# Attention times a gated FFN on one Trainium2 core: features in rows for x, gate and result

## Chip, cores and metric

One core of a Trainium2 chip. The metric is the device time of one execution in microseconds (us): the median of three runs for the kernel before, and beside it one profiled execution, from which all durations below are taken. PE is TensorE (PEld its weight loads), DVE is VectorE, ACT is ScalarE, POOL is GpSimd, SP is SyncE, which does nothing here but issue DMAs.

## What is computed

x is [8, 512, 256]: B = 8 sequences of T = 512 tokens with E = 256 features.

```python
xn = layernorm(x)                              # over the features, no weights
q, k, v = split(xn @ in_proj_w.T)              # 16 heads of 16
q, k = rope(q), rope(k)
mask = (delta >= 0) & (delta < 250)            # causal, a window of 250
s = softmax(where(mask, q k^T / 4, min)) v @ out_proj_w.T
h = relu(s0 * [xn, -xn] @ W0) * 2              # W0, W1, W2 hold +1 and -1
h = relu(s1 * h @ W1) * 2                      # 256 -> 1024 -> 1024 -> 256
g = silu(s2 * h @ W2)
result = x + s * g
```

## The kernel before

**Tiles.** A tile has 128 rows (partitions). A sequence is NT = 4 token tiles; its features are EC = 2 chunks of 128. Matmuls put the token axis or the feature axis in the rows of their result according to which operand is the stationary one. Before the change x is loaded with tokens in rows (load_x, L106), four tiles of 128 tokens by 256 features.

**One batch.**
- stats (L231): per token tile a bn_stats and a bn_aggr on DVE give mean and variance; DVE adds EPS and POOL takes the power -1/2 (L240).
- norm (L247): DVE writes xn = (x - mean) * rstd, both of them one number per row.
- turn_x (L255): two TensorE transposes per token tile (L268) bring xn into features-in-rows; DVE copies it to xT (L280; ACT in batch 0, L278), ACT writes the scaled fp16 part xh (L281), DVE the remainder xl (L284).
- project (L302): k and q, each in parts a and b, from xT [2 chunks, 512 tokens] into PSUM, times cosine and sine on DVE (L319), rotated on POOL (L339), split into a high and a low part (split_hi L353 on ACT, split_lo L359 on DVE), both written to DRAM and read back in another arrangement (stack, L366) with four heads in the rows. project_v (L288) gives v with tokens in rows.
- layer (L399): the two wide FFN layers, L415. Each product is one fp16 and one fp32r matmul per chunk, 512 columns; the result is split again by ACT (L426) and DVE (L424).
- last (L429): z = h2 @ W2 with tokens in rows, four tiles of 128x256, 16 matmuls each; DVE scales it into gate (L467). gate_ready (L493): exp on ACT, plus one on POOL, reciprocal on DVE (L503), product on POOL.
- attention: nine steps per batch. A step computes scores (L605), takes exp on ACT (L624), masks on POOL (L640, L647) and multiplies the step before with v (L679). keep (L690) gathers a group of heads, invert and divide (L752 on) make the quotients.
- project_o (L778): att @ w_o per token tile; x is loaded a second time (xr, L787), DVE multiplies by gate (L804), POOL adds xr (L809), SP stores.

**Order.** Nothing is left to a scheduler. Each piece of work is a triple (place, cost, function). run (L212) sorts the pieces by place, calls them in that order, and keeps a clock that is the sum of the costs of pieces so far. A function may return follow-ups with a delay; they are called when the clock has passed their due time. So a place in units of SEQ = 42 per batch says where in the instruction streams of all engines a piece stands, and a delay says how many units of TensorE work lie between. Each engine, SP too, runs its stream strictly in order. prepare (L374) gives the places for the next batch's stats, norm, x, k, q and v; ffn (L534) those of the layers; last_at and late (L512, L519) those of z and of project_o; attention (L720) puts the nine steps among the pieces by cost and places the stacks.

**Buffers.** ps_m has three PSUM banks, shared by transposes, projections, FFN tiles, z and project_o in rotation; ps_s has two buffers for scores (two banks each), ps_o one. xT, xh and xl, as well as the tile for part b of q and k, are single. The last batch (b = 7) does its second layer in two halves of 256 tokens, so that the first half's z can come early.

**The start.** Loads of x, the weights and the rope table go out at 0.8 to 4.4 us; kb0, kb1 and kb2 are the boolean weights as bytes, from which w0, w1 and w2 are made in two precisions on DVE, ACT and POOL (make_w0 L169, make_w1 L174, make_w2 L182). warm (L206) runs idle matmuls to keep TensorE busy until the first real ones.

**The end.** project_o of the last batch stands for token tiles 0 and 1 at unit 40, within the second half of the second layer, and for tiles 2 and 3 after z. The last tile is multiplied on POOL and DVE and stored by SP (out_of_psum, L792).

Of the kernel before, what the change touches and what calls it, by code (L numbers as in the profile page):

```python
# [34 lines left out]
def tile_attention_times_gated_ffn(  # L35
    ctx: ExitStack,
    tc: tile.TileContext,
    x: bass.AP,
    w_qkv: bass.AP,
# [6 lines left out]
    out: bass.AP,  # L46
):

# [75 lines left out]
    nc.scalar.dma_start(wqkv_sb, w_qkv.rearrange("(c p) f -> p c f", p=P))  # L124
# [18 lines left out]
    counts = const.tile([P, 3 * B], F32, name="counts")  # L143

# [24 lines left out]
    def make_w0(c):  # L169

        nc.vector.tensor_tensor(w0["h"][:, c], kb0[:, c], kb0[:, EC + c], ALU.subtract)
        nc.scalar.copy(w0["l"][:, c], w0["h"][:, c])
# [58 lines left out]
    def stats(b):  # L231
        st = states[b] = {}
        mv = small.tile([P, NT, 2], F32, tag="mv", name=f"mv_{b}")
        rstd = small.tile([P, NT], F32, tag="rstd", name=f"rstd_{b}")
        for t in range(NT):
            bn = small.tile([P, 6], F32, tag="bn", name=f"bn_{b}_{t}")
            nc.vector.bn_stats(bn, xs[b, t])
            nc.vector.bn_aggr(mv[:, t, :], bn)
        nc.vector.tensor_scalar(rstd, mv[:, :, 1], EPS, None, ALU.add)
        nc.gpsimd.tensor_tensor(rstd, rstd, minus_half, ALU.pow)  # L240
        nc.vector.scalar_tensor_tensor(
            mv[:, :, 1], mv[:, :, 1], LEAST_VAR, ones, ALU.is_ge, ALU.mult,
            accum_out=counts[:, 2 * B + b : 2 * B + b + 1],
        )
        st["mv"], st["rstd"] = mv, rstd

    def norm(b, t):  # L247
        st = states[b]
        xn = st["xn", t] = work.tile([P, E], F32, tag="xn", name=f"xn_{b}_{t}")
        nc.vector.tensor_scalar(  # L250
            xn, xs[b, t], st["mv"][:, t, 0:1], st["rstd"][:, t : t + 1],
            ALU.subtract, ALU.mult,
        )

    def turn_x(b, t, plain=False):  # L255

        st = states[b]
        xn = st.pop(("xn", t))
# [7 lines left out]
        pt = ps_m.tile([P, EC, P], F32, tag="mm", name=f"xnT_ps_{b}_{t}")  # L266
# [8 lines left out]
        def parts_():  # L275
            xT = st["xT"][:, :, ts(t, P)]
            if b == 0:
                nc.scalar.copy(xT, pt)  # L278
            else:
                nc.vector.tensor_copy(xT, pt)  # L280
            nc.scalar.mul(hi, pt, sgnx)  # L281

        def low():
            nc.vector.scalar_tensor_tensor(lo, pt, sgnx, hi, ALU.mult, ALU.subtract)  # L284

        return [(0.0, parts_), (0.5, low)]
# [15 lines left out]
    def project(b, what, part):  # L302
        st = states[b]
        col = E * "qk".index(what) + P * "ab".index(part)
        ps = ps_m.tile([P, T], F32, tag="mm", name=f"{what}{part}_ps_{b}")
# [11 lines left out]

        def times(i):
            nc.vector.tensor_tensor(  # L319
                m[:, i], ps, rope_sb[:, i if part == "a" else 1 - i], ALU.mult  # L320
            )

        def both():
            times(0)
            times(1)
            if part == "b":
                return [
                    (1.4, lambda: rotate(b, what)),
                    (4.0 if b else 7.0, lambda: split_hi(b, what)),
                    (5.1 if b else 8.2, lambda: split_lo(b, what)),  # L330
                ]

        return [(0.0, both)]
# [40 lines left out]
    def prepare(b, plain=False):  # L374

        if b == 0:
            at = dict(stats=-40, norm=-38, x=-36, k=0, q=3, v=9.2)
            dx, dp, dv = 1.0, 1.5, 1.5
        else:

            at = dict(stats=9 if b > 1 else 12, norm=14.5, x=16.5, k=22, q=25, v=SEQ + 0.6)
            dx, dp, dv = 1.5, 1.5, 1.0
            at = {n: SEQ * (b - 1) + f for n, f in at.items()}
        out = [(at["stats"], 0, lambda: stats(b))]
        for t in range(NT):
            out += [
                (at["norm"] + dx * t, 0, lambda t=t: norm(b, t)),
                (at["x"] + dx * t, 0.25, lambda t=t: turn_x(b, t, plain)),
                (at["v"] + dv * t, 0.87, lambda t=t: project_v(b, t)),
            ]  # L390
# [38 lines left out]
    def last(b, t, how):  # L429
        st = states[b]  # L430
        pz = ps_m.tile([P, E], F32, tag="mm", name=f"z_ps_{b}_{t}")
        if how == "at once":
            for c in range(NF1):
                nc.tensor.matmul(
                    pz, st["h2p"][:, c, ts(t, P)], w2["l"][:, c].bitcast(F32),
                    start=(c == 0), stop=(c == NF1 - 1),
                )
        else:
            for p in "hl":
                for c in range(NF1):  # L440
                    nc.tensor.matmul(  # L441
                        pz, st["h2" + p][:, c, ts(t, P)], w2[p][:, c],
                        start=(c == 0 and p == "h"), stop=(c == NF1 - 1 and p == "l"),
                    )
        gate = st["gate", t] = outs.tile([P, E], F32, tag=f"gate{t}", name=f"gate_{b}_{t}")
        if how == "final":
            den = denominator(b, t)

            def ends():
                nc.scalar.activation(den, pz, AF.Exp, scale=scales[:, 1:2])  # L450
                nc.vector.tensor_scalar(gate, pz, scales[:, 0:1], None, ALU.mult)
                return [(0.3, add)]

            def add():
                nc.scalar.activation(den, den, AF.Identity, bias=1.0)
                return [(0.3, invert_)]

            def invert_():
                nc.vector.reciprocal(den, den)
                if t + 1 < NT:  # L460
                    nc.gpsimd.tensor_tensor(gate, gate, den, ALU.mult)
                st["den"] = den
# [3 lines left out]
        def scale():  # L466
            nc.vector.tensor_scalar(gate, pz, scales[:, 0:1], None, ALU.mult)  # L467
            if how != "later":
                return [(0.5 if t == 0 else 4.5, lambda: gate_ready(b, t))]
# [20 lines left out]
    def denominator(b, t):  # L490
        return work.tile([P, E], F32, tag="den", name=f"den_{b}_{t}")

    def gate_ready(b, t):  # L493
        st = states[b]
        gate, den = st["gate", t], denominator(b, t)
        nc.scalar.activation(den, gate, AF.Exp, scale=-1.0)

        def add():
            nc.gpsimd.tensor_scalar(den, den, 1.0, None, ALU.add)  # L499
            return [(0.9, invert_)]  # L500

        def invert_():
            nc.vector.reciprocal(den, den)  # L503
            return [(1.8, lambda: nc.gpsimd.tensor_tensor(gate, gate, den, ALU.mult))]
# [7 lines left out]
    def last_at(b, t):  # L512

        if b + 1 < B:
            return SEQ * (b + 1) + 2 * L1 * (t + 1) + L3 * t
        half = t // 2
        return SEQ * b + NF0 * L1 + NT * L3 + HALF * (half + 1) - 2 * L3 + L3 * (t % 2)

    def late(b, t):  # L519

        if b + 1 == B and t >= NT // 2:
            return last_at(b, NT - 1) + L3 + 0.9 * (t - NT // 2)
        if b + 1 == B:
            return SEQ * b + 40.0 + 0.9 * t
        return SEQ * (b + 1) + (32.0 + 3.2 * t if b + 2 < B else 18.0 + 2.5 * t)

    def finish_ffn(b, t, how):
        quick.add(last_at(b, t))
        out = [(last_at(b, t), L3, lambda: last(b, t, how))]
        if how == "later":  # L530
            out.append((late(b, t) - 4.0, 0, lambda: gate_ready(b, t)))
        return out

    def ffn(b):  # L534
# [3 lines left out]
        for f in range(NF0):  # L538
# [3 lines left out]
            if f % 2 and b > 0:  # L542
                now += L3
# [176 lines left out]
    def attention(b, among):  # L720
# [17 lines left out]
        for g in range(NG):  # L738

            at = times[used[g - 2][-1]] + 0.01 if g > 1 else first - (10.0 if b else 2.0)  # L740
# [37 lines left out]
    def project_o(b, t, final=False):  # L778
        st = states[b]
        pp = ps_m.tile([P, E], F32, tag="mm", name=f"att_ps_{b}_{t}")  # L780
        for c in range(EC):
            nc.tensor.matmul(  # L782
                pp, st["V", c][:, ts(t, P)], wo_sb[:, c, :],
                start=(c == 0), stop=(c == EC - 1),
            )
        xr = work.tile([P, E], F32, tag="xr", name=f"xr_{b}_{t}")
        nc.sync.dma_start(xr, x[b, ts(t, P), :])  # L787
        st["xr", t] = xr
        if final and t + 1 == NT:
            att = work.tile([P, E], F32, tag="xn", name=f"att_{b}_{t}")  # L790

            def out_of_psum():  # L792
                y, den = st["gate", t], st["den"]
                nc.scalar.copy(att, pp)
                nc.gpsimd.tensor_tensor(y, y, att, ALU.mult)
                nc.vector.tensor_tensor(y, y, den, ALU.mult)
                nc.vector.tensor_tensor(y, y, xr, ALU.add)
# [206 lines left out]
```

## Time and profile before

| | |
|---|---|
| runs | 627.25, 627.94, 629.54 us; median 627.94 |
| profiled execution | 628.36 us, of which the span of the profile is 626.6 |
| granted TensorE clock, mean | 0.996 |
| busy DVE, ACT, POOL | 394.1, 299.7, 316.2 us |
| transposes xnT_ps (L268) | 64, median 273 ns each as recorded |
| xn (L250) | 32, mean 752 ns |
| xT copies on DVE (L280) | 28, mean 418 ns |
| z_ps (L441) | 512 matmuls of 256 columns |
| att_ps (L782) | 128 matmuls of 256 columns |
| DMA in all | 67.20 MB, mean 107 GB/s |

The recorded duration of a matmul includes its way through the array, and successive ones overlap; the time that TensorE spends on one is read from the distance of two starts, or from the chain of work. A wait is put down to the semaphore that came last.

### The profile page before, as it was taken

How to read it: one execution, taken by the hardware profiler on the slowest of the kernel's cores; microseconds unless marked ns; L12 is line 12 of the kernel's file. 1: busy time of each engine (PE TensorE's matmuls, PEld its weight loads, DVE VectorE, ACT ScalarE, POOL GpSimd, SP SyncE). 2: the span in 40 equal slices, each digit the busy share in tenths (PEclk: the TensorE clock that was granted, in tenths of full speed). 3: DMA queues.
4: the chain of work that ended last, by engine and by line, in shares of the span. 5: the costliest groups of instructions: out<-in, count | busy, mean ns of one | idle time of the engine just before them, and what ended most of it. 6: DMA issues, size and time to landing. Idle time of an engine off the chain costs nothing.

```text
span 626.6 us, 12051 instructions
## 1 busy us (share of the span) xinstructions
PE 608.6 (97%) x4842; PEld 398.4 (64%) x4842; DVE 394.1 (63%) x667; ACT 299.7 (48%) x441; POOL 316.2 (50%) x409
## 2 busy tenths in 40 slices
PE   8899999999999999999999999999999999999994
PEld 6455576556665567655676566765676556767793
DVE  6773535667575774766658576485665668456573
ACT  4566655534554445545354454453444544564411
POOL 2954542456533655427634366235662356638641
PEclk9999999999999999999999999999999999999998
DMA  9352721116311263114421252412532116230101
GB/s 273 117 197 95 260 85 51 51 68 216 122 51 51 87 208 110 52 51 172 139 93 51 75 214 76 143 33 86 208 94 88 51 69 227 77 109 19 53 18 48
DMA packets 38193, 67.20 MB, mean 107 GB/s; under 512 B 5104, under 2 KB 19184, under 8 KB 38128
## 3 DMA queue, kind: packets, MB, share of 16 engines
q1 hardware_dynamic: 36384, 64.24, 30.5%
q10 hardware_dynamic: 1744, 2.10, 1.0%
q8 instruction: 40, 0.66, 0.4%
q14 instruction: 25, 0.20, 0.1%
HBM read 36.96 MB, written 29.36 MB: 106 GB/s over the span
## 4 chain that ended last, share of the span: by engine, by line
PE 85%; DVE 5%; POOL 3%; DMA 3%; ACT 2%; issue 1%; SPq 0%; POOLq 0%; ACTq 0%; DVEq 0%
PE h_ps L415 41%; PE po L679 11%; PE z_ps L441 9%; PE sc L605 8%; PE v_ps L292 4%; PE att_ps L782 4%; PE qa_ps L307 2%; PE kb_ps L307 2%; PE qb_ps L307 2%; DMA kb<-in_k_dram 2%; PE ka_ps L307 2%; PE xnT_ps L268 1%; DVE den L503 1%; DVE h2l L424 1%; DVE xn L250 1%
## 5 line engine op out<-in xcount | busy, mean ns | idle before, releaser
L624 ACT ACTIVATE p<-sc 128x1024 f32<-128x1024 f32 (+2 forms) x144 | 138.5, 1013 | 75.0 <-PE sc L605 41.0
L415 PE MATMUL h_ps<-h1l,w1l_sb 128*128 128x512 f32 (+1 forms) x576 | 144.2, 392 | 0.0
L640 POOL TENSOR_SCALAR_AFFINE_SELECT p<-p 128x512 f32<-128x512 f32 x128 | 90.3, 711 | 104.0 <-ACT p L624 104.0
L415 PE MATMUL h_ps<-h1h,w1h_sb 128*128 128x512 f16 (+1 forms) x576 | 123.0, 356 | 0.5 <-ACT v_pad L299 0.5
L415 PEld LDWEIGHTS h_ps<-h1l,w1l_sb 128*128 128x128 f32 x576 | 99.5, 188 | 25.7 <-issue 6.8
L426 ACT ACTIVATE h2h<-h_ps 128x512 f16<-128x512 f32 (+1 forms) x72 | 39.6, 550 | 140.3 <-PE h_ps L415 140.2
L415 PEld LDWEIGHTS <-w1h_sb 128*128 128x128 f16 x576 | 51.5, 98 | 55.1 <-issue 13.4
L679 PE MATMUL po<-p,v_pad 128*32 128x378 f32 (+4 forms) x1216 | 77.2, 372 | 1.3 <-DVE S L703 1.1
L647 POOL TENSOR_SCALAR_AFFINE_SELECT p<-p 128x512 f32<-128x512 f32 (+1 forms) x96 | 50.0, 521 | 54.6 <-ACT p L624 49.7
L424 DVE SCALAR_TENSOR_TENSOR h2l<-h_ps,h2h 128x512 fp32r<-128x512 f32 (+1 forms) x72 | 44.3, 617 | 48.5 <-ACT h2h L426 48.5
L503 DVE RECIPROCAL den<-den 128x256 f32<-128x256 f32 x30 | 52.5, 1752 | 28.2 <-POOL den L499 28.1
L424 DVE SCALAR_TENSOR_TENSOR h1l<-h_ps,h1h 128x512 fp32r<-128x512 f32 x64 | 42.4, 675 | 34.8 <-ACT h1h L426 34.8
L605 PEld LDWEIGHTS sc<-q,k 32*128 32x128 f32 x1216 | 44.1, 184 | 26.1 <-issue 15.0
L754 DVE RECIPROCAL S<-S 128x128 f32<-128x128 f32 x64 | 58.9, 933 | 0.0
L426 ACT ACTIVATE h1h<-h_ps 128x512 f16<-128x512 f32 x64 | 38.2, 597 | 41.8 <-PE h_ps L415 41.2
L605 PE MATMUL sc<-q,k 32*128 32x378 f32 (+4 forms) x1216 | 57.2, 306 | 0.0
L415 PE MATMUL h_ps<-xl,w0l_sb 128*128 128x512 f32 x128 | 52.5, 491 | 0.0
L679 PEld LDWEIGHTS po<-p,v_pad 128*32 128x32 f32 x1216 | 31.3, 109 | 30.8 <-issue 16.2
L809 POOL TENSOR_TENSOR gate<-gate,xr 128x256 f32<-128x256 f32 x31 | 25.1, 810 | 46.8 <-DMA xr<-in_x_dram 41.2
L441 PE MATMUL z_ps<-w2l_sb,h2l 128*128 128x256 f32 x256 | 38.3, 291 | 0.4 <-DVE h2l L424 0.4
L415 PE MATMUL h_ps<-xh,w0h_sb 128*128 128x512 f16 x128 | 38.6, 383 | 0.0
L339 POOL TENSOR_TENSOR m_ka<-m_ka,m_kb 128x512 f32<-128x512 f32 x16 | 20.1, 1278 | 30.3 <-DVE m_kb L319 30.3
(97 smaller groups left out, 811.0 us busy)
## 6 DMA issues: line engine op xcount, KB each, us to landing
q<-dq SPq DMA_DIRECT2D x64, 256.0 KB, 3.6
dq<-qh SPq DMA_DIRECT2D x16, 512.0 KB, 3.4
dq<-m_qa SPq DMA_DIRECT2D x16, 512.0 KB, 5.0
k<-dk SPq DMA_DIRECT2D x32, 256.0 KB, 2.8
dk<-kh SPq DMA_DIRECT2D x8, 512.0 KB, 2.6
dk<-m_ka SPq DMA_DIRECT2D x8, 512.0 KB, 2.6
xr<-in_x_dram SPq DMA_DIRECT2D x32, 128.0 KB, 2.8
out_dram<-gate SPq DMA_DIRECT2D x32, 128.0 KB, 1.7
```

The costliest lines, as they stand in the source:

```text
L307: nc.tensor.matmul(ps, wqkv_sb[:, c, ds(col, P)], st["xT"][:, c, :], start=(c == 0), stop=(c == EC - 1),)
L415: nc.tensor.matmul(ph, w[p][:, c, ts(f, P)], st[src + p][:, c, cols], start=(k == 0), stop=(k == n - 1),)
L424: nc.vector.scalar_tensor_tensor(lo, ph, 0.0, hi, ALU.max, ALU.subtract)
L426: high = lambda: nc.scalar.activation(hi, ph, AF.Relu)
L441: nc.tensor.matmul(pz, st["h2" + p][:, c, ts(t, P)], w2[p][:, c], start=(c == 0 and p == "h"), stop=(c == NF1 - 1 and p == "l"),)
L503: nc.vector.reciprocal(den, den)
L605: nc.tensor.matmul(sc[r // 2][:, r % 2, ds(off, n)], st["k0", g][row, ts(j, P)], st[f"q{turn}", g][row, ds(j * P + first, n)], start=(turn ...
L624: nc.scalar.activation(p[:, 2 * half : 2 * half + 2, :n], sc[half][:, :, :n], AF.Exp, scale=D ** -0.5,)
L640: nc.gpsimd.affine_select(out=block, in_=block, compare_op=ALU.is_ge, fill=0.0, base=0, pattern=[[0, 4], [1, P]], channel_multiplier=-1,)
L647: nc.gpsimd.affine_select(out=block, in_=block, compare_op=ALU.is_ge, fill=0.0, base=-1, pattern=[[0, 4], [-1, beyond]], channel_multiplier=1,
L679: nc.tensor.matmul(po[32 * r : 32 * r + 32, ds(j * P + first, n)], v_columns(j, g, r), p_[:, r, ds(off, n)], start=(j == 0), stop=(done an ...
L754: nc.vector.reciprocal(part, part)
```

## The change

The host also hands over x transposed (x_t, [8, 256, 512]) and takes the result transposed (out_t); it does no arithmetic.

- Batches 1 to 7: x is still loaded with tokens in rows for stats, but xn and its transposes are gone. raw x^T is loaded straight into xT (load_xT, SP). The moments of all tokens, one column each of rstd and mean for four token tiles, lie in a tile of 128x32; lay_down turns it on DVE in blocks of 32x32 and writes it to DRAM in four DMAs, lay_over reads it back so that each of 128 rows holds rstd and mean of all 512 tokens (512 KB). norm_turned then subtracts and multiplies in place on DVE, per chunk of 128x512, and makes xh (ACT) and xl (DVE).
- Batch 0 still transposes; it normalises in place, takes its statistics for two tiles at a time, uses the score banks for two of the transposes and for q's projections, and copies all of xT on ACT before it makes the parts. wqkv is loaded in three pieces, k's first; signs, w0 and the warming matmuls have other places and numbers.
- z, gate, the residual and the projection by w_o have features in rows: per batch two tiles of 128 features by 512 tokens for four of 128 tokens by 256 features; in the last batch four of 128x256. The stationary and the moving operand change sides. Residuals are loaded at gate_ready, from x_t.
- In the last batch all four projections by w_o stand behind z's last tile; the reciprocal there is followed by one operation that scales z and multiplies; the ends of the four tiles are shared among POOL, DVE and two DMA queues.

The core of the diff (the parts of norm and turn_x for batch 0, host lines and the fallback for extreme values are left out):

```diff
-    nc.scalar.dma_start(wqkv_sb, w_qkv.rearrange("(c p) f -> p c f", p=P))
+    for n in (1, 0, 2):
+        nc.scalar.dma_start(
+            wqkv_sb[:, :, ts(n, E)], w_qkv[:, ts(n, E)].rearrange("(c p) f -> p c f", p=P)
+        )
...
     def stats(b):
         st = states[b] = {}
+        n = 2 if b == 0 else NT
+        mv = st["mv"] = moments[:, b % 2, : 3 * NT].rearrange("p (i t) -> p t i", t=NT)
         for t in range(NT):
             bn = small.tile([P, 6], F32, tag="bn", name=f"bn_{b}_{t}")
             nc.vector.bn_stats(bn, xs[b, t])
+            nc.vector.bn_aggr(mv[:, t, 1:3], bn)
+            if (t + 1) % n == 0:
+                part = mv[:, t + 1 - n : t + 1, 0]
+                nc.vector.tensor_scalar(part, mv[:, t + 1 - n : t + 1, 2], EPS, None, ALU.add)
+                nc.gpsimd.tensor_tensor(part, part, minus_half[:, :n], ALU.pow)
...
+    def load_xT(b):
+        raw_xT[b] = one.tile([P, EC, T], F32, tag="xT", name=f"xT_{b}")
+        nc.sync.dma_start(raw_xT[b], x_t[b].rearrange("(c p) t -> p c t", p=P))
+
+    def lay_down(b):
+        turned_ = small.tile([P, 32], F32, tag="turned", name=f"moments_{b}")
+        nc.vector.transpose(turned_, moments[:, b % 2])
+        d = states[b]["moments"] = dram.tile([2 * NT, P], F32, tag="moments", name=f"d_{b}")
+        for q in range(P // 32):
+            nc.sync.dma_start(d[:, ts(q, 32)], turned_[32 * q : 32 * q + 2 * NT, :])
+
+    def lay_over(b):
+        st = states[b]
+        of_all = st["of_all"] = turned.tile(
+            [P, 2, T], F32, tag="mb", name=f"of_all_{b}", bufs=1
+        )
+        d = st["moments"].rearrange("(i t) p -> i (t p)", i=2)
+        nc.sync.dma_start(of_all, d.partition_broadcast(P))
+
+    def norm_turned(b, c):
...
+        xT = st["xT"][:, c]
+        for i, op in ((1, ALU.subtract), (0, ALU.mult)):
+            nc.vector.tensor_tensor(xT, xT, st["of_all"][:, i], op)
+        hi, lo = (st["x" + p][:, c] for p in "hl")
+        def low():
+            nc.vector.scalar_tensor_tensor(lo, xT, sgnx, hi, ALU.mult, ALU.subtract)
+        return [(0.8, lambda: nc.scalar.mul(hi, xT, sgnx)), (1.3, low)]
...
     def project(b, what, part):
-        ps = ps_m.tile([P, T], F32, tag="mm", name=f"{what}{part}_ps_{b}")
+        if b == 0 and what == "q":
+            ps = ps_s.tile([P, 2, T], F32, tag="sc", name=f"{what}{part}_ps_{b}")[:, 0]
+        else:
+            ps = ps_m.tile([P, T], F32, tag="mm", name=f"{what}{part}_ps_{b}")
...
-        return [(0.0, both)]
+        return [(1.5 if b == 0 and what + part == "qb" else 0.0, both)]
...
     def prepare(b, plain=False):
-            at = dict(stats=9 if b > 1 else 12, norm=14.5, x=16.5, k=22, q=25, v=SEQ + 0.6)
-            dx, dp, dv = 1.5, 1.5, 1.0
+            at = dict(load=9, stats=9, down=10.5, over=12, norm=16.8, k=21.8, q=24.8, v=SEQ + 0.6)
+            if b == 1:
+                at.update(load=18.65, stats=12, down=18.64, over=19.5, norm=23, k=27, q=29)
+            dp, dv = 1.5, 1.0
...
     def last(b, u, how):
-                        pz, st["h2" + p][:, c, ts(t, P)], w2[p][:, c],
+                        pz, w2[p][:, c, ts(f, P)], st["h2" + p][:, c, cols],
...
-                return [(0.5 if t == 0 else 4.5, lambda: gate_ready(b, t))]
+                return [(7.5 if u == 0 else 11.0, lambda: gate_ready(b, u))]
...
     def last_at(b, u):
         if b + 1 < B:
-            return SEQ * (b + 1) + 2 * L1 * (t + 1) + L3 * t
+            return SEQ * (b + 1) + 4 * L1 * (u + 1) + 2 * L3 * u
...
     def late(b, u):
         if b + 1 == B:
-            return SEQ * b + 40.0 + 0.9 * t
-        return SEQ * (b + 1) + (32.0 + 3.2 * t if b + 2 < B else 18.0 + 2.5 * t)
+            return last_at(b, 3) + L3 + 0.9 * u
+        return SEQ * (b + 1) + (33.5 + 6.4 * u if b + 2 < B else 19.2 + 5.0 * u)
...
-            at = times[used[g - 2][-1]] + 0.01 if g > 1 else first - (10.0 if b else 2.0)
+            at = times[used[g - 2][-1]] + 0.01 if g > 1 else first - (
+                2.0 if b == 0 else 4.0 if b == 1 else 9.0
+            )
...
     def project_o(b, u, final=False):
-                pp, st["V", c][:, ts(t, P)], wo_sb[:, c, :],
+                pp, wo_sb[:, c, ts(f, P)], st["V", c][:, cols],
...
-        xr = work.tile([P, E], F32, tag="xr", name=f"xr_{b}_{t}")
-        nc.sync.dma_start(xr, x[b, ts(t, P), :])
...
-        (-38.5, 0, signs), (-40.5, 0, lambda: warm(12)), (-34.5, 0, lambda: warm(3)),
-        (-32.5, 0, lambda: warm(5)),
+        (-34.6, 0, signs), (-40.5, 0, lambda: warm(9)), (-34.7, 0, lambda: warm(2)),
+        (-32.5, 0, lambda: warm(1)), (-31.0, 0, lambda: enough(0)),
+        (-32.7, 0, lambda: first_parts(0, 1)),
```

## The prediction

> **What bounds the kernel now.** I read the busy shares first, then the steady batches by window, then the chain of work that ended last in one batch, and last the two ends.
>
> ```profile
> PE 608.6 (97%) x4842; PEld 398.4 (64%) x4842; DVE 394.1 (63%) x667; ACT 299.7 (48%) x441; POOL 316.2 (50%) x409
> ```
> ```profile
> 16.00:34.00 18.00, 14.65 (x58) 8.31 (x57) 13.38 (x27) 10.31 (x17) 16.63 (x13) 1.00 0.34 135
> ...
> 243.50:318.40 74.90, 74.76 (x587) 47.98 (x586) 49.38 (x81) 35.64 (x52) 37.29 (x49) 1.00 0.33 112
> ...
> 543.20:613.00 69.80, 68.28 (x680) 55.04 (x677) 41.53 (x70) 29.16 (x50) 36.43 (x49) 1.00 0.18 58
> ```
>
> The windows give length, then busy time of PE, weight loads, DVE, ACT and POOL. A batch in the middle lasts 74.9 us and TensorE is busy for 74.8 of them at full clock; DVE has 26 us to spare, ACT 39, POOL 37. So there TensorE alone sets the time, and each microsecond taken from it counts until another chain comes up. In the last batch it idles 1.5 us. Between 16 and 34 us it idles 3.4, for these reasons:
>
> ```profile
> PE v_ps L292 <- DVE h1l L424: 1.6, 2, 0.8
> PE v_ps L292 <- DVE m_qb L319: 1.3, 1, 1.3
> ```
>
> The chain within one batch, around the part that the change removes:
>
> ```profile
> 261.18 3.69 PE h_ps L415 x16
> 264.87 0.23 PE xnT_ps L268 x2
> 265.10 0.02 issue
> 265.12 0.42 DVE xT L280
> 265.55 0.71 DVE xn L250
> 266.26 0.61 DVE h2l L424
> 266.87 0.04 issue
> 266.91 0.45 PE xnT_ps L268 x2
> 267.36 0.03 issue
> 267.39 0.41 PE xnT_ps L268 x2
> 267.80 1.87 PE h_ps L415 x8
> 269.67 0.22 PE xnT_ps L268 x2
> 269.89 0.68 PE sc L605 x16
> ```
>
> From 264.87 to 269.89 are 5.02 us. In them TensorE did 16 matmuls of one h_ps tile (3.69 in the first row); 1.33 us are left for the eight transposes. Their own part is about 0.22 x 4 = 0.9, the rest waits for the copies and for xn.
>
> **The Trainium skill.** "TensorE: Matmul & The Clock Gate", Part 4 (PE-mode transpose), gives about 275 ns for a transpose inside a kernel; the trace has a median of 273, but starts are 0.11 us apart, and the chain, not the duration, prices them. "VectorE: DVE Perf Modes", The three transpose paths: VectorE turns 32x32 blocks only, 311 ns for 128x128; no row of before shows it. The same page, Two Vector instructions with no wait between them, says that the second SBUF read interface is shared with GpSimd; the trace agrees in that the L363 subtraction (128x1024, both inputs in SBUF) took 1.22 us at one place and 2.11 at another. "DMA: Bandwidth & Descriptors", Anatomy of one DMA, puts a fixed cost of some 2 us on a transfer; here a 128 KB store took 1.7 us to land.
>
> **Transposes.** For batches 1 to 7 turn_x goes: 7 x 1.33 = **9.3 us** off TensorE. The bounds are 7 x 0.9 = 6.3 (if the stalls reappear elsewhere) and 9.3.
>
> **Normalising.** DVE loses four norms (4 x 0.75), four copies (4 x 0.42) and four lows (4 x 0.475), 6.6 us a batch. It gets four tensor_tensor of 128x512 with both inputs in SBUF: half of L363's 1.22 to 2.11, so 0.6 to 1.05 each, 2.4 to 4.2; two lows at 0.68; a transpose of 128x32, 0.1 to 0.31 (I take 0.2). ACT has two scalings at about 0.6 for four at 0.474. Both engines get less to do. It is latency that has to be examined: before k's projection can start, the chain is stats, pow, turn, four writes, broadcast, normalise. In the times of the middle batch: stats stand now ahead of the second z tile and can begin after the h1l that ended at 254.6; they took 2.6, so 257.2; pow 1.05 and the turn, 258.8 with the waits between. SP issued nothing between 254.5 and 270.4, so nothing is queued there behind the new waits: four issues at 0.33 and 1.7 to land, 261.8. The broadcast writes 512 KB; stores and loads of 512 KB landed in 2.6 (dk<-kh) to 5.0 (dq<-m_qa), and I take 3.8: there at about 266, ends 264.7 and 267.1. The four operations with an h2l between them end at 268 to 272. ka_ps began at 274.03, now 1.33 earlier, 272.7. Slack is 1 to 4.5 us, about 2.7 in the middle: cost **0**, at worst about 1 a batch. While DVE stands at norm_turned, only the h2l of f=0 is queued behind it; it was executed at 266.2 and its PSUM bank is needed again by ka (three banks), so the wait has room. The x_t load (512 KB) is issued three units before the broadcast and overlaps stats. For batch 1 the places are later (19.5 and 23, k at 27), with k moved by 5 units; the stacks come at 38, and rotation to stack took some 18 us here (qb_ps 16.45, stack 35.4): fits, 0.
>
> **Larger tiles.** Two z tiles of 512 columns for four of 256: 16 matmuls took 1.83 to 1.92 at 256 columns and 3.69 at 512, so two for one saves 0 to 0.15; I take 0. The projection by w_o: 379 ns duration at 256, 216 ns from start to start, against 430 at 512: 0. POOL, DVE and ACT do half as many operations of twice the length, hidden under TensorE; if that cover goes it is in the last batch, where I allow plus or minus 1. Residuals are now loaded at gate_ready, so POOL's wait of 41.2 us in total for xr disappears: off the path, 0.
>
> **The start.** The weight kb1 lands at 15.04; POOL makes two w1l parts (to 17.6), turns k (to 20.1), and only then can m_qb be written, since its tile is single. v_ps stood behind m_qb by its PSUM bank. Now q lies in the score banks and m_qb comes 1.5 units later, behind the first h1l. I follow it: m_qb still 20.1 to 21.4, then h1l of f=1 to 22.1 and of f=2 to 22.7; the cast of k moves from 24.0 to about 21, and the subtraction L363 from 25.1 to 22.7. From there DVE's order is unchanged and it is nearly full, so the first w1 matmul moves from 33.2 to about 31.3: **1.9 us**. Bounds: 0.3, if kb1 lands later because three issues for wqkv stand before it on ACT's queue (two more at 0.45 us), or if VectorE is held by w0's wait for kb0 (9.9); 3 if all idle time goes. k's weights first and the split stats let TensorE start about 1.5 earlier than 11.06, which h1's wait eats; fewer warming matmuls cost at most some 0.5 for the same reason.
>
> **The end.**
>
> ```profile
> 613.99 0.48 ACT den L450
> ...
> 619.30 0.83 DVE gate L797
> ```
>
> These are the first and the last step of the chain behind z's third tile, which ends at 613.9; DVE then needs until 620.13, and the last store is issued at 620.6. Now all four projections by w_o come after z, so both z tiles come 2 x 0.86 = 1.7 earlier. After z: exp and add 0.9, reciprocal 1.75, product 0.48, one product for u=0 0.4, again 1.75 and 0.48, an add of 0.4 to 0.8, product and add of u=3 0.8 to 1.2: 7.0 to 7.8, so 7.4 against 6.7 to the last issue. 1.7 - 0.7 = 1.0, and I take **0.8** (ends -0.3 and 1.5).
>
> **Sum.** 9.3 + 1.9 + 0.8 = 12.0, less 0.5 for waits that I can't place: 11.5. The profiled execution took 628.36 (span 626.6): 616.9. The median of the runs is 0.42 lower: **616.5**. From the ends: 6.3 + 0.3 - 0.3 - 1 = 5.3 gives 622.6, and 9.3 + 3 + 1.5 + 1 = 14.8 gives 613.1.
>
> **Rivals.**
> - Late moments, small (0.10): the broadcast lands near 7.5 us after issue, 3.7 later than taken; less the slack of 2.7 that is 1 us in each of seven batches: 616.5 + 7 = 623.5. For it: the writes, the landing and the read are a serial chain through one queue. Against it: SP is empty then.
> - Late moments, large, on the slower side (0.06): all 128 rows read the same 4 KB in DRAM. If that takes 9 us, ka_ps waits 9 - 3.8 - 2.7 = 2.5 us in seven batches, 17.5 in all: 634. It decides from a landing of some 8.2 us (11.5 / 7 = 1.65 beyond the slack). For it: no transfer here reads one place 128 times, and x took up to 8.1 once. Against it: 512 KB otherwise need 2.6 to 5.0, and bursts reach 273 GB/s.
> - Work was hidden (0.08): TensorE shows no waits, but ACT, POOL and DVE may be only just ahead in the attention steps, and without the transposes po waits for masks. Half of 9.3 returns: 621. Against it: POOL waits for ACT 104 us in L640 alone, and po hardly waits (0.2).
> - The forecast's own case (0.76).
>
> **Chances.** About 0.5% (3 us) is what a measurement here can tell from no change; faster means below 624.8. Forecast, hidden work and half of the small late case lie there: 0.76 + 0.08 + 0.05 = 0.89; the other half is within 0.5%, 0.05; slower 0.06. The range leaves out the large case, most of the small one and a little at either side: 613.0 to 621.5.
>
> **What would show it.** In the profile after: eight transposes in all; a period from z_ps to z_ps of 73.6 us for 74.9; ka_ps not waiting for DVE xT; DVE idle before norm_turned on the broadcast; the first w1 matmul near 31.3; last store issue about 0.8 earlier relative to the last matmul of h_ps. A wait of TensorE in ka_ps in each batch would prove me wrong, as would a period of 74.5 or more.

## The result and the profile after

The kernel after takes 619.07 us in the median of four runs (617.28 to 620.87), the kernel before 628.29 beside it (627.25 to 629.54). The ratio is 0.9846, with a 95% interval of 0.9826 to 0.9866: faster by 1.5%, in the forecast range and 2.6 us above the forecast itself. The profiled execution took 617.83, its span is 616.1.

The busy times of the whole span, the windows (length, then busy time of PE, weight loads, DVE, ACT and POOL with their counts, clock, DMA share and GB/s) and TensorE's waits (total, times, longest), all of the kernel after:

```profile
PE 598.1 (97%) x4490; PEld 367.5 (60%) x4490; DVE 381.7 (62%) x606; ACT 294.9 (48%) x414; POOL 308.8 (50%) x368
```
```profile
16.00:32.00 16.00, 13.36 (x55) 7.66 (x54) 13.31 (x24) 9.75 (x16) 16.00 (x12) 1.00 0.38 149
38.43:89.24 50.81, 46.79 (x402) 25.57 (x402) 21.04 (x30) 28.07 (x34) 22.24 (x33) 0.97 0.41 145
245.39:318.63 73.24, 73.24 (x540) 43.45 (x537) 46.95 (x72) 34.98 (x49) 36.27 (x43) 1.00 0.35 123
```
```profile
PE sc L712 <- ACT p L731: 2.2, 2, 1.6
PE v_ps L358 <- DVE h1l L506: 2.0, 3, 1.4
...
PE po L786 <- POOL p L754: 0.8, 2, 0.6
```

A middle batch is now 73.24 us long and TensorE is busy for all of it: there the change does what it says. But the attention of batch 0 (38.43 to 89.24) has 4.0 us without TensorE work and a mean clock of 0.97. In the kernel before, the same stretch, from the first scores of batch 0 to those of batch 1, was 44.99 us long with TensorE busy for 44.82:

```profile
41.29:86.28 44.99, 44.82 (x403) 25.04 (x402) 18.29 (x28) 27.85 (x34) 21.51 (x33) 1.00 0.46 154
```

So I cut both spans at the same events on TensorE:

| stretch | before, us | after, us | difference | forecast |
|---|---|---|---|---|
| start to the first w1 matmul | 33.19 | 31.15 | -2.04 | -1.9 |
| first w1 matmul to first scores of batch 1 | 53.09 | 58.09 | **+5.00** | -1.3 |
| six periods, first scores of batch 1 to those of batch 7 | 449.91 | 439.47 | -10.44 | 6 x -1.33 = -8.0 |
| first scores of batch 7 to the third z tile | 75.71 | 73.04 | -2.67 | -1.7 |
| third z tile to the issue of the last store | 8.71 | 9.11 | +0.40 | +0.7 |
| that issue to the end of the span | 5.99 | 5.24 | -0.75 | 0 |
| sum | 626.6 | 616.1 | -10.5 | |

One row has the wrong sign. (Two more profiles of the same code up to the first scores of batch 1, those of e4b and e5 below, have 56.75 and 57.35 us in this row, so it is +3.7 to +5.0.) The chain of waits of the kernel after, in that place (start, length, what):

```profile
38.08 3.51 DMA d<-moments
41.58 0.02 issue
41.60 4.58 DMA of_all<-d
...
47.03 0.70 DVE xT L301
47.73 0.02 issue
47.76 0.72 ACT xh L307
48.48 0.48 ACT h2h L508
48.96 1.80 ACT p L731 x2
50.76 0.06 issue
50.82 0.87 POOL p L754
...
53.93 3.23 PE ka_ps L376 x4
```

Read it downwards: two DRAM transfers take 8.1 us, DVE normalises, ACT makes xh, and only behind xh comes the exp (p) of an attention step. TensorE needs that p. The timeline shows the same on the engines; in brackets stands how long the engine had been idle, and for whom:

```profile
47.76 0.72 ACT L307 ACTIVATE xh<-xT,sgnx 128x512 f16<-128x512 f32 x1 [4.54 <-DVE xT L301]
48.39 0.58 ACT L508 ACTIVATE h2h<-h_ps 128x512 f16<-128x512 f32 x1
48.86 1.89 ACT L731 ACTIVATE p<-sc 128x1000 f32<-128x1000 f32 x2
49.91 0.33 PE L712 MATMUL sc<-q,k 32*128 32x128 f32 x2 [1.63 <-ACT p L731]
50.80 0.84 PE L712 MATMUL sc<-q,k 32*128 32x128 f32 x14 [0.57 <-ACT p L731]
52.96 0.97 PE L786 MATMUL po<-p,v_pad 128*32 128x256 f32 x8 [0.60 <-POOL p L754]
53.86 3.30 PE L376 MATMUL ka_ps<-xT,wqkv_sb 128*128 128x512 f32 x4
```

ACT executes in order. It stands 4.54 us at xh; the exp whose scores were ready from 43.6 runs at 48.86. TensorE waits 1.63, 0.57 and 0.60, and after that the four matmuls of ka_ps take 3.30 us instead of 1.88: the granted clock is 0.50 from 53.2 to 56.5. In the middle batch, the place that the forecast had followed, the same wait is harmless:

```profile
258.76 1.30 SPq L281 DMA_DIRECT2D d<-moments  x4
...
262.06 0.34 SPq L290 DMA_DIRECT2D of_all<-d  x1
...
265.84 1.42 DVE L301 TENSOR_TENSOR xT<-xT,of_all 128x512 f32<-128x512 f32 x2 [5.28 <-DMA of_all<-d]
...
267.29 0.72 ACT L307 ACTIVATE xh<-xT,sgnx 128x512 f16<-128x512 f32 x1 [2.79 <-DVE xT L301]
...
268.72 1.41 DVE L301 TENSOR_TENSOR xT<-xT,of_all 128x512 f32<-128x512 f32 x2
...
271.43 1.88 PE L376 MATMUL ka_ps<-xT,wqkv_sb 128*128 128x512 f32 x4
```

The moments are there at 265.8, xT is complete at 270.1 and needed at 271.43. ACT stands 2.79 us at xh, but nothing behind it is due. This batch is the slowest of the six in that: counted from the start of the second z tile, it uses the moments after 10.5 us, the other five after 8.9 to 9.5. And where the chain of before ran through transposes and copies, the chain after is TensorE alone:

```profile
260.19 7.28 PE h_ps L497 x32
267.46 0.67 PE sc L712 x13
268.13 1.63 PE po L786 x24
269.76 1.83 PE h_ps L497 x8
271.59 1.72 PE ka_ps L376 x4
```

### The profile page after: what moved, and what is told of

Read it like the earlier page. It is cut to its first block, busy times and chain, and to the rows that moved or that the text cites. A ratio compares the mean times of both kernels' runs of the same rounds, so it can differ in the third digit from the quotient of the medians.

```text
span 616.1 us, 11176 instructions
## 1 busy us (share of the span) xinstructions
PE 598.1 (97%) x4490; PEld 367.5 (60%) x4490; DVE 381.7 (62%) x606; ACT 294.9 (48%) x414; POOL 308.8 (50%) x368
## 4 chain that ended last, share of the span: by engine, by line
PE 91%; DVE 4%; POOL 2%; DMA 1%; ACT 1%; issue 1%; SPq 0%; DVEq 0%; ACTq 0%; POOLq 0%
PE h_ps L497 44%; PE po L786 11%; PE z_ps L551 9%; PE sc L712 8%; PE v_ps L358 4%; PE att_ps L895 4%; PE ka_ps L376 3%; PE qb_ps L376 2%; PE qa_ps L376 2%; PE kb_ps L376 2%; PE warm L224 1%; DMA of_all<-d 1%; ACT p L731 1%; DMA d<-moments 1%; DVE den L568 1%
## 5 line engine op out<-in xcount | busy, mean ns | idle before, releaser
L747 POOL TENSOR_SCALAR_AFFINE_SELECT p<-p 128x512 f32<-128x512 f32 x128 | 91.6, 722 | 136.2 <-ACT p L731 135.7
L497 PE MATMUL h_ps<-h1l,w1l_sb 128*128 128x512 f32 (+1 forms) x576 | 146.5, 396 | 0.0
L612 DVE RECIPROCAL den<-den 128x256 f32<-128x256 f32 (+1 forms) x32 | 52.6, 1645 | 25.2 <-POOL den L607 25.2
L506 DVE SCALAR_TENSOR_TENSOR h1l<-h_ps,h1h 128x512 fp32r<-128x512 f32 x64 | 42.7, 679 | 24.7 <-ACT h1h L508 24.7
L863 DVE RECIPROCAL S<-S 128x128 f32<-128x128 f32 x64 | 57.4, 918 | 0.0
L508 ACT ACTIVATE h1h<-h_ps 128x512 f16<-128x512 f32 x64 | 38.1, 598 | 21.5 <-PE h_ps L497 21.4
L301 DVE TENSOR_TENSOR xT<-xT,of_all 128x512 f32<-128x512 f32 x28 | 22.5, 805 | 32.2 <-DMA of_all<-d 31.8
L551 PE MATMUL z_ps<-h2l,w2l_sb 128*128 128x512 f32 (+1 forms) x144 | 35.8, 390 | 0.0
L358 PE MATMUL v_ps<-wqkv_sb,xT 128*128 128x256 f32 x128 | 33.1, 381 | 2.0 <-DVE h1l L506 2.0
```

What stands on the lines that cost most here:

```text
L358: nc.tensor.matmul(v.rearrange("p n s d -> p (n s d)"), st["xT"][:, c, ts(t, P)], wqkv_sb[:, c, 2 * E :], start=(c == 0), stop=(c == EC - 1),)
L497: nc.tensor.matmul(ph, w[p][:, c, ts(f, P)], st[src + p][:, c, cols], start=(k == 0), stop=(k == n - 1),)
L506: nc.vector.scalar_tensor_tensor(lo, ph, 0.0, hi, ALU.max, ALU.subtract)
L508: high = lambda: nc.scalar.activation(hi, ph, AF.Relu)
L551: nc.tensor.matmul(pz, w2[p][:, c, ts(f, P)], st["h2" + p][:, c, cols], start=(c == 0 and p == "h"), stop=(c == NF1 - 1 and p == "l"),)
L612: nc.vector.reciprocal(part, part)
```

## The experiments

**The theory** (A in the expectations): batch 1's xh, queued on ACT ahead of an exp, holds the attention of batch 0, and that costs some 5 us once. Its rivals stand in the expectations of e1 and e2b.

**e1, batch 1's xh later.** The one change is when xh and xl of batch 1 are given to the queues; xl is not on the chain above.

```diff
-        return [(0.8, lambda: nc.scalar.mul(hi, xT, sgnx)), (1.3, low)]
+        hi_at, lo_at = (4.0, 5.0) if b == 1 else (0.8, 1.3)
+        return [(hi_at, lambda: nc.scalar.mul(hi, xT, sgnx)), (lo_at, low)]
```

> The changed kernel, with one thing different: for batch 1 alone, the scaling of xT into xh on ScalarE and the remainder xl stand 4.0 and 5.0 units after norm_turned instead of 0.8 and 1.3. Theory A (the late moments of batch 1 stop ScalarE, because xh stands ahead of h2h and of the exp of step 1, and TensorE then waits for exp and masks and loses its full clock): ScalarE no longer stands still from 43.2 to 47.8, TensorE has no wait before the scores of step 2, the first scores of batch 1 begin at about 84.2 instead of 89.2, and the time is about 614 (span 611). Theory B (VectorE, stopped at norm_turned until the moments land, holds the PSUM banks): nothing changes, 619, since VectorE's order is the same.

Measured: 614.14 us (613.64 to 614.68), ratio to the kernel before 0.9771 (0.9755 to 0.9788). The timeline of e1 in the same place, and its window from the first scores of batch 0 to those of batch 1:

```profile
44.46 1.90 ACT L732 ACTIVATE p<-sc 128x1000 f32<-128x1000 f32 x2
...
46.37 1.73 DVE L301 TENSOR_TENSOR xT<-xT,of_all 128x512 f32<-128x512 f32 x2 [5.69 <-DMA of_all<-d]
...
48.13 0.72 ACT L308 ACTIVATE xh<-xT,sgnx 128x512 f16<-128x512 f32 x1 [1.78 <-DVE xT L301]
...
49.03 0.85 PE L713 MATMUL sc<-q,k 32*128 32x128 f32 x16
...
50.79 1.98 PE L377 MATMUL ka_ps<-xT,wqkv_sb 128*128 128x512 f32 x4
```
```profile
39.26:84.88 45.62, 44.46 (x402) 24.99 (x401) 21.09 (x30) 28.22 (x34) 22.47 (x33) 1.00 0.47 160
```

The exp now stands ahead of xh and runs at 44.46. The moments land as late as ever (DVE waits 5.69), and it costs nothing: the scores don't wait, ka_ps takes 1.98, the window is 5.2 us shorter and the clock 1.00. So A holds, and B falls. Giving the parts of one batch to the queues later is worth 4.9 us of 619.

**e2b, batch 1 normalised later.** Everything of norm_turned moves, DVE's part too.

```diff
-                at.update(load=18.65, stats=12, down=18.64, over=19.5, norm=23, k=27, q=29)
+                at.update(load=18.65, stats=12, down=18.64, over=19.5, norm=25.2, k=27, q=29)
```

> The changed kernel with batch 1's norm_turned at 25.2 instead of 23, nothing else: VectorE and ScalarE reach it one layer tile later, about when the moments land (46). Theory A (ScalarE stopped at xh ahead of the exp) expects what moving xh and xl alone gave: 614, first scores of batch 1 near 85. Theory C (xh in place is harmless, what counted in the run before was something else that its delay shifted) leaves it at 619.

Measured: 614.11 us (613.38 to 614.54), ratio 0.977 (0.9753 to 0.9786): the same as e1. From the first w1 matmul to the first scores of batch 1 it takes 53.3 us, e1 52.9, the kernel after 58.1. Once ACT is free for the exp it doesn't matter where DVE stands, as A says; C falls.

**e3, q of batch 0 back in the three shared banks.** The start was the second part of the forecast. Here q's projection goes to the banks that v_ps uses, and m_qb follows at once; the other changes of the start stay.

```diff
-        if b == 0 and what == "q":
+        if False:
...
-        return [(1.5 if b == 0 and what + part == "qb" else 0.0, both)]
+        return [(0.0, both)]
```

> The changed kernel with q's projections of batch 0 back in the three shared PSUM banks and the product of qb back at delay 0. If the start's 2.0 us come from freeing v_ps and the first h1l from the product of qb, the first w1 matmul moves from 31.15 back to about 33 and the time rises by about 2 to 621. If they come from the earlier transposes and weights of k, it stays at 31.2 and 619.

Measured: 622.23 us (620.76 to 623.76), ratio 0.989 (0.9873 to 0.9907), so 3.2 more than the kernel after. The first w1 matmul comes at 38.12, far later than expected and than in either kernel. From TensorE's timeline of e3:

```profile
21.73 2.07 PE L358 MATMUL v_ps<-wqkv_sb,xT 128*128 128x256 f32 x4 [3.54 <-DVE m_qb L390]
...
32.87 0.59 PE L497 MATMUL h_ps<-xh,w0h_sb 128*128 128x512 f16 x2 [2.48 <-ACT v_pad L365]
...
37.15 1.13 PE L358 MATMUL v_ps<-wqkv_sb,xT 128*128 128x256 f32 x4 [2.32 <-DVE h1l L506]
38.12 3.27 PE L497 MATMUL h_ps<-h1h,w1h_sb 128*128 128x512 f16 x8
```

v_ps waits 3.54 for m_qb: the wait that the forecast named. The granted clock is 0.50 from 21.5 to 24.7 and again from 38.5 to 41.8, which adds to the delay. With the new order of k and q the old banks and the old delay are worse than the old kernel was (33.19), so the parts of the start belong together; their values can't be added up, and this run doesn't say which of the two that it puts back counts more.

**e4b, z in halves of 256 columns.** The forecast put the wide z tiles at nothing. Batches 0 to 6 compute each z tile in two sets of matmuls of half the width.

```diff
-            for p in "hl":
+            wide = T if b + 1 < B else T // 2
+            for at in range(0, wide, T // 2):
+                for p in "hl":
...
-                        pz, w2[p][:, c, ts(f, P)], st["h2" + p][:, c, cols],
+                            pz[:, at : at + T // 2], w2[p][:, c, ts(f, P)],
+                            st["h2" + p][:, c, ds(cols.start + at, T // 2)],
```

> The changed kernel with each z tile of 512 columns computed in two halves of 256 columns, so 32 matmuls for 16, everything else the same. If wide tiles are worth what a batch gains beyond the transposes (1.74 measured less 1.33), the period from batch to batch goes from 73.25 to about 73.6 and the time rises by 2 to 3. If width is worth nothing (the prediction's 0), period and time stay: 73.25, 619.

Measured: 618.22 us (616.91 to 619.5), ratio 0.9832 (0.981 to 0.9854). The period is 73.35 for 73.25: 0.1 us a batch.

**e5, the moments later.** For batches 2 to 7 stats, the writes and the broadcast are placed later. It asks how much room the DRAM trip has.

```diff
-            at = dict(load=9, stats=9, down=10.5, over=12, norm=16.8, k=21.8, q=24.8, v=SEQ + 0.6)
+            at = dict(load=9, stats=10.8, down=12.1, over=13.1, norm=16.8, k=21.8, q=24.8, v=SEQ + 0.6)
```

> The changed kernel with stats, lay_down and lay_over of batches 2 to 7 at 10.8, 12.1 and 13.1 instead of 9, 10.5 and 12: the second z tile's scaling and a reciprocal then stand ahead of the statistics, and the moments land about 3 us later, near 268.8 in the middle batch instead of 265.8. The slack measured there is 1.3 (xT ready at 270.1, ka_ps at 271.4). If the rival of late moments is priced rightly, ka_ps waits about 1.7 us in each of six batches: period 75, time near 629. If VectorE and ScalarE can make up for it, the time stays within 2 of 619.

Measured: 630.0 us in eleven of twelve runs (626.13 to 635.23; the twelfth took 636.15), ratio 1.0022 (0.9997 to 1.0046). In five of the six batches the moments are used 13.9 to 14.3 us after the start of the second z tile, instead of 8.9 to 9.5. This delay of 4.3 to 5.3 us, not the 3 expected, costs 1.4 to 2.1 us a period, so there was room for about 3 us and not for 1.3; that the time came close to the 629 named is these two errors together. In the remaining batch, the slow one above, the delay was 5.7 (259.55 to 275.80; before it 255.34 to 265.84) and the period 6.3 longer; the timeline of e5 shows why:

```profile
275.80 1.42 DVE L301 TENSOR_TENSOR xT<-xT,of_all 128x512 f32<-128x512 f32 x2 [7.25 <-DMA of_all<-d]
...
277.87 1.20 PE L376 MATMUL ka_ps<-xT,wqkv_sb 128*128 128x512 f32 x2 [2.07 <-DVE h2l L506]
...
280.13 2.07 PE L376 MATMUL ka_ps<-xT,wqkv_sb 128*128 128x512 f32 x2 [1.07 <-DVE xT L301]
...
281.22 4.40 PE L497 MATMUL h_ps<-h1l,w1l_sb 128*128 128x512 f32 x8
```

TensorE waits 2.07 and 1.07, and the next eight matmuls take 4.40 us; they take 2.4 elsewhere. The granted clock is 0.50 from 278.8 to 285.6, so the halving began after the first wait, before the second. The time of this kernel goes with the clock: the five runs with a mean clock of 0.995 or more took 626.1 to 629.6, the seven below that 630.0 or more. Here the rival of late moments is real: beyond that room, they eat the whole gain of the change.

**e6, eight idle transposes per batch at the old places.** e1 with transposes whose result nobody reads, each pair in a PSUM tile of its own. This adds work that the result doesn't use.

```diff
+    def idle_turn(b, t):
+        pt = ps_m.tile([P, EC, P], F32, tag="mm", name=f"idle_{b}_{t}")
+        for c in range(EC):
+            nc.tensor.transpose(pt[:, c, :], xs[b, t][:, ts(c, P)], ident)
...
+            if "over" in at:
+                out.append((
+                    SEQ * (b - 1) + 16.5 + 1.5 * t, 0.25, lambda t=t: idle_turn(b, t)
+                ))
```

> The version with xh and xl of batch 1 moved (614.1), plus eight transposes per batch for batches 1 to 7 at the places where they stood in the kernel before, into the shared PSUM banks, of x as loaded, and read by nobody: TensorE does the removed work again, without waiting for anyone. If the own time of the transposes is 0.9 a batch, seven batches cost 6.3: 620.4, period 74.1. If it is 1.33 (what the chain gave with the waits), 9.3: 623.4, period 74.6.

Measured: 629.7 us (628.5 to 631.94), ratio 1.0028 (1.0018 to 1.0038). The period is 75.6 to 76.1 for 73.25, more than either figure. TensorE's waits in e6:

```profile
PE idle L353 <- DVE h2l L516: 7.9, 6, 1.7
```

Each pair takes one of three PSUM banks. The bank is free once DVE has read it for h2l, and h2l stands on DVE behind norm_turned, which waits for the moments. So e6 prices transposes with bank waits of the new order, not the transposes, and another form was needed.

**e8, the same eight in one bank.** They stand together between the projections of k and of q, in one tile.

```diff
+        if "over" in at:
+            out.append((at["k"] + 2.6, 1.0, lambda: idle_turns(b)))
```

> The version of e1, and in each of batches 1 to 7 eight TensorE transposes whose result nobody reads, all eight into one PSUM tile between the projections of k and of q (work is added that the result does not use). It prices the transposes alone, with one turn of the three PSUM banks for four and no wait for a copy. If eight transposes cost their start distances only, 8 x 0.11 = 0.9 us a batch: period 74.1 for 73.25, time 614.1 + 6.3 = 620.4. If the whole gain of 1.74 a batch that the kernel after showed is the price of the transposes themselves: period 75.0, time 626. If they are worth the 1.33 of the forecast without any wait: period 74.6, time 623.4.

Measured: 619.56 us (619.17 to 620.05), ratio 0.9847 (0.983 to 0.9865). The period is 74.12, 0.87 more than without. All eight, from TensorE's timeline:

```profile
274.59 1.04 PE L354 MATMUL idle<-ident,x 128*128 128x128 f32 x8
```

So transposes cost 0.87 us a batch by themselves, the forecast's lower figure (0.9). Where the rest of the 1.74 went can be read from a ledger: the time from each start on TensorE to the next, added up by kind over the six periods of the kernels before and after. In it the transposes of before took 1.18 a batch, 0.3 more than alone. The other 0.56 lies elsewhere: z 0.10, v 0.14, po 0.06, the projection by w_o and the h_ps matmuls together 0.25. These sums blur by some 0.2 where two kinds meet (e10), so the split is a reading, not a test.

**e10 and e1 again, the projection by w_o in matmuls of 256 columns**, beside e1.

```diff
-                pp, wo_sb[:, c, ts(f, P)], st["V", c][:, cols],
+                    pp[:, at : at + T // 2], wo_sb[:, c, ts(f, P)],
+                    st["V", c][:, ds(cols.start + at, T // 2)],
```

> The version of e1, with the projection by w_o of batches 0 to 6 in matmuls of 256 columns (16 a batch, for 8 of 512). It tests a row of the ledger made from the starts of TensorE's instructions: these projections took 3.26 us a batch before and 3.03 after. If width is the reason, the period goes from 73.25 to 73.47 and the time from 614.1 to about 615.5 (7 x 0.22 = 1.5 more). The forecast on record had 0 for it: then the period stays at 73.25 and the time at 614.1, and the 0.22 came with the place of the matmuls among the others.

> The version of e1 once more, beside e10 on the same chip: about 614.1, period 73.25. Its first w1 matmul is looked at too: the start of the kernel is that of the kernel after, in which it stood at 31.15; in e1 it stood at 31.98. If the start is steady it comes at 31.1 to 31.3 or 31.98 again; if single profiles scatter there, anywhere from 31 to 32.5.

Measured: e10 614.89 us (613.53 to 615.15), ratio 0.9775 (0.9758 to 0.9793); e1 613.71 (613.31 to 614.24), ratio 0.9766 (0.975 to 0.9782). The intervals overlap, and the periods are 73.26 and 73.24. From start to start the projections do take 3.25 us for 3.03, but the h_ps matmuls behind them take 37.63 for 37.83: the difference lies at the border between two groups and cancels. The row of the ledger that I had built on it fell; the forecast's 0 stands. e1 again had its first w1 matmul at 31.53. The eleven profiles with the start of the kernel after (all but e3, that kernel's own among them) have it from 31.15 to 32.68, with a median of 32.14.

**e7, q's low part out of the way of the masks.** In e1 TensorE still waits 0.97 us for masks of step 7, three of which take 2.97 us on POOL, the first beside DVE's subtraction of q's high part.

```diff
+        if b == 1 and what == "q":
+            lo_after = 6.4
```

> The version of e1 (batch 1's fp16 x on ScalarE later), and in it the subtraction that makes the low part of batch 1's q on VectorE 1.3 units later, so that it doesn't lie beside the three masks of step 7 on GpSimd. Theory: those masks took 0.99 us each for 0.64 because both engines read SBUF with two operands at once, and the TensorE wait of 0.97 us for them (po, near 75 us) is that contention. Then the masks return to 0.64 each, the wait is 0 to 0.2, and the span falls from 612.0 to about 611.1; time about 613.3 for 614.1. Rival: the masks take 0.99 for a reason of their own; then they stay at 2.97 for three, the wait stays at 1.0, and the time stays at 614.1 (or rises, if the stacks of batch 1 come late).

Measured: 613.86 us (613.52 to 614.47), ratio 0.9757 (0.9742 to 0.9772). The subtraction and POOL's masks in e1, the masks in e7, then TensorE in e7:

```profile
73.46 1.23 DVE L436 TENSOR_TENSOR m_qa<-m_qa,qh 128x1024 fp32r<-128x1024 f32 x1 [4.22 <-ACT qh L429]
73.54 2.97 POOL L748 TENSOR_SCALAR_AFFINE_SELECT p<-p 128x512 f32<-128x512 f32 x3
```
```profile
73.72 1.22 POOL L750 TENSOR_SCALAR_AFFINE_SELECT p<-p 128x512 f32<-128x512 f32 x2
...
76.05 0.64 POOL L750 TENSOR_SCALAR_AFFINE_SELECT p<-p 128x512 f32<-128x512 f32 x1 [1.11 <-ACT p L734]
```
```profile
84.75 0.62 PE L715 MATMUL sc<-q,k 32*128 32x378 f32 x12 [0.26 <-DMA q<-dq]
```

The wait is gone, so the two operations do contend. But 0.99 was a mean that hid what happens: in e1 the first of the three masks, which starts while the subtraction runs, takes 1.63 us and ends 0.50 after it, and the other two take 0.63 each. The time doesn't follow: the low part of q goes to DRAM later, the first scores of batch 1 now wait for q, that period is 73.77 us for 73.25, and the median is within the scatter of e1's. About half of the gain was turned into a new wait; what is left of it is too small to be told from nothing.

**e9, the very last store on SyncE.** e1 with the old queue for the last store.

```diff
-            adder, queue = (nc.vector, nc.scalar) if very_last else (nc.gpsimd, nc.sync)
+            adder, queue = (nc.vector, nc.sync) if very_last else (nc.gpsimd, nc.sync)
```

> The version of e1, but the very last store is issued on SyncE again, behind the stores ahead of it, as in the kernel before. Theory: of the 2.2 us by which the end beat the forecast, 0.75 is this queue. Then last issue to span end goes from about 5.2 back to about 6.0 us, and the time from 614.1 to about 614.9. Rival: the store lands as late either way, and the shorter landing came from elsewhere (fewer bytes under way): 614.1, difference below 0.3.

Measured: 614.79 us (614.16 to 616.11), ratio 0.9777 (0.9761 to 0.9793), overlapping with e1. The issue comes 0.6 us later (607.11 for 606.52), and from issue to end it takes 5.3 us, not 6.0. The same distance with ACT's queue is 5.2 in the kernel after, 5.4 in e1, 5.9 in e7 and 6.3 in e10. So the 0.75 in my table lies within the scatter of single profiles, and the queue's worth stays open below some 0.6 us.

## Why the prediction was right and where it failed

**Transposes: right in mechanism, a batch's gain too low.** Eight are left, DVE waits for the broadcast (31.8 us in seven waits), ka_ps doesn't wait in the middle batches. The period was to be 73.6 and is 73.25. A batch gains 1.74 instead of 1.33. The runs split it: 0.87 for the transposes themselves (e8), 0.1 for the width of z (e4b), nothing for the width of the projection (e10); about 0.8 is left, of which the ledger puts some 0.3 at the transposes and the rest at other matmuls, whose order changed too. That part is not tested. The 1.33 itself was a little high for the transposes (1.18 in the ledger): it subtracted 3.69 for an h_ps tile whose 16 matmuls take 3.81 in the mean. What was missing is gain at the other matmuls, which the forecast had at 0.

**Moments in the middle batches: right, the exact time by luck.** The broadcast was guessed to land at 266 and was used at 265.84, and its transfer took 3.75 us for the 3.8 taken; but that batch is the slowest of the six, the others have their moments 1.0 to 1.6 us sooner. The room of 2.7 us was about 3 in those (e5). The large case of late moments was a true danger: 4.3 to 5.7 us of delay ate the gain. Of the rival that work was hidden under the transposes nothing shows: TensorE has no idle time in a middle batch.

**Moments of batch 1: "fits, 0" is the step that failed.** It cost 6.0 us: 58.09 for the 53.09 of before less the 1.02 which the transposes took in that stretch. The working looked at what comes after (k at 27, stacks at 38) and, for a middle batch, at DVE ("only the h2l of f=0 is queued behind it"). It never asked what is queued behind xh on ACT, which norm_turned issues 0.8 units later and which waits for DVE, which waits for the DMA. In batch 0 that was the exp of a step about to be used, and the moments came later than elsewhere: the four small writes took 3.51 us to land and the broadcast 4.58. e1 takes away this one order and gets back 5.2 us of the 6.0 in the stretch, 4.9 in the median; a wait of 0.97 for the masks is still there (e7). With the two other profiles of that stretch the 6.0 is 4.7 to 6.0.

**The start: right in mechanism, its size open.** The cast of k moved from 24.02 to 20.97 (forecast about 21) and the subtraction behind it from 25.09 to 22.04 (22.7). The single profiles give -2.04 for the forecast's -1.9, but the profile after is the earliest of the eleven; with their median it is 32.14 - 33.19 = -1.05, and of the kernel before I have one profile. That is also a part of why the profiled execution after lies 1.2 us below its median.

**The end: mis-sized.** Up to the issue of the last store it gained 2.3 us (-2.67 + 0.40) where I took 0.8. The two projections that moved behind z took 1.73 us out of the stretch ahead of it, as forecast (1.7); a wait of z_ps for h2l of 0.4 us went, which I had not followed; some 0.5 is spread over z, po and the projections of batch 6 and has no tested cause; and the tail grew by 0.4, not 0.7. The allowance of 0.5 for waits that I couldn't place was far too small in sum and in the wrong batch.

So the forecast came near by three misses that partly cancel: 6.0 lost in batch 0, some 2.2 more won at the transposes and the matmuls around them (1.02 + 10.44 for 9.3), and some 1.5 more at the end; that the sum fell into the range is in part luck. Mend the first and the kernel takes 614 us (e1, e1 again, e2b), below the forecast: the change is worth 2.3%, and a third of that was lost by one place in ACT's queue.

## What to carry to other kernels

When an operation starts to wait for a DMA, follow not only its own queue: list what each of its consumers on other engines is placed ahead of, since a consumer that is issued early hands the wait on to all that stand behind it. Do this for the first and the last round separately: they have other orders, and here the first had slower transfers too (9.3 us from the first write to use, 5.5 to 7.1 in the middle). To price a removed operation, put it back idle, but where it takes no shared buffer, or the buffer's waits are priced with it.

## What the runs showed of the hardware

- **Half clock after short waits, but not after all of them.** ka_ps took 3.30 us for 1.88 after waits of 1.63, 0.57 and 0.60 us within 5.6 us, its weight loads 0.34 us for 0.19, at a granted clock of 0.50. In e4b, in the same place, only waits of 0.25, 0.57 and 0.60 stood before it (0.50 from 53.8 to 57.0), in e5 one of 2.07. The Trainium skill, "TensorE: Matmul & The Clock Gate", What's actually happening, puts the halving after an idle window of about 3.4 us; none of these waits is that long. Yet a wait of 2.48 us in e3 (to 32.87) left the clock at 1.00. So the length of the waits alone doesn't decide; what does is not shown here.
- **DVE and POOL in SBUF.** A mask of 128x512 on POOL takes 0.63 us, and 1.63 when it starts 0.08 after a DVE subtraction of 128x1024 with both inputs in SBUF; the subtraction keeps its 1.23 (e1). In the kernel before, where POOL had started first, such a subtraction took 2.11 (25.09), and 1.22 with POOL idle (60.15). So in these cases the one that came later paid. The Trainium skill, "VectorE: DVE Perf Modes", Two Vector instructions with no wait between them, names a second SBUF read interface of DVE that is shared with GpSimd; the traces agree.
- **A small trip through DRAM.** Four writes of 1 KB and a read that lays 4 KB over 128 rows (512 KB) took 5.5 to 6.1 us from the first issue to use in five of six middle batches, 7.1 in the one shown (258.76 to 265.84) and 9.3 in batch 0. From the first write's issue to that of the broadcast it was 2.2 in the five, 3.3 in the one shown and 4.6 in batch 0; the broadcast landed in 3.3 to 3.9, in batch 0 in 4.6. Why the one batch is slower stays open; it is so in nine of the twelve profiles that have this trip.
- **Transposes.** Eight of 128x128 on TensorE have a median of 273 ns each, and add 0.87 us in all: 0.11 each, since they overlap. The turn of 128x32 on DVE took 0.15 to 0.20 us, for the 0.2 taken.
